# A graph network's edge loop: attribute products grouped behind the first transposes, message sums in one run behind the second product

## The chip, the cores and the metric

The kernel runs on one core of a Trainium2 chip. The metric is the device time of one execution in microseconds (us), the median of several runs. A core has five engines that each work through their own instructions in order and wait for one another by semaphores: PE (TensorE, matrix products), ACT (ScalarE, functions and copies), DVE (VectorE, elementwise work), POOL (GpSimd, which issues the gathers here) and SP (which issues plain transfers). PEld is TensorE's weight load, which runs beside its products. Products land in PSUM, a small memory from which ACT and DVE read.

## The reference

Four graph layers run one after the other on 4096 nodes of 512 features and 65,536 edges sorted by destination; each adds its result to the node features. Layer 2 passes messages along the edges, and its edge part is what matters here:

```python
def mish(x):
    return x * jnp.tanh(jax.nn.softplus(x))
edge_feat = jnp.concatenate([x[src], x[dst], edge_attr], axis=-1)
h = mish(edge_feat @ W1 + b1)
messages = mish(h @ W2 + b2)
agg = jax.ops.segment_sum(messages, dst, num_segments=x.shape[0])
```

`x` is normalized and rectified before; `edge_attr` has 64 numbers an edge. `agg` then goes through another small network over the nodes. All of it is fp32.

## The kernel before

The product with W1 is split by its three inputs. Two tables over the nodes, `ptab` (source part) and `qtab` (destination part, with b1), are made before the loop. The loop (function `messages`, L937 to L1089) then works through 128 groups of 512 edges. A group is four blocks (j = 0 to 3) of 128 edges, one edge on each partition. For a group it does the following:

- `fetch_rows` (L941) gathers four blocks of `ptab` rows by source into the tile `pg`, and `add_rows` (L947) gathers the `qtab` rows by destination on top of them. POOL issues these eight gathers. `pg` has four buffers.
- `fetch_attributes` (L905) loads the 64 attributes of the edges into `eg`, through SP's queue. `eg` has four buffers.
- `turn_attributes` (L954) transposes the attributes on PE, two blocks at a time (L957), and ACT copies them to `et` (L959).
- `attribute_products` (L962) multiplies one block's attributes by their rows of W1, `w1e`. The product has only 64 rows of depth, so blocks 0 and 2 use one half of TensorE's rows and blocks 1 and 3 the other (L967). DVE adds the result to the gathered rows (L1050, L1057).
- The first mish is worked out as h * cos(2 arctan(sigmoid(-h))), the cosine as a sine: Sigmoid (L1005), Arctan (L1024) and Sin (L1069) on ACT into the tile `qg`, and a multiplication on DVE in two halves (L1070, L1079). The first group has its own function for this, `first_mish` (L997). Sigmoid and Sin need different function tables, so ACT loads a table twice a group.
- `turn_h(j)` (L971) transposes one block of the result in four pieces (L974), and ACT copies it to `h_t` (L976).
- `second_product` (L979) multiplies it by W2 (`product`, L401) into `m_ps`. DVE adds b2 and so makes `z` (L1036, L1053, L1067, L1077). Products 0 to 3 below are those of blocks 0 to 3.
- The second mish is the same on `z`, with the tile `t` (L1028, L1046, L1063 on ACT, L1064, L1074 on DVE).
- `in_parts` (L984) splits the messages into two parts that a faster matrix format can hold, on DVE (L987, L988). `one_hots` (L404) compares each edge's local destination with 0 to 127 (L407).
- `add_messages` (L991) sums the messages by destination: a product of the one-hot matrix with the parts, two products a block (L994), into `sum_ps`. `add_window` (L420) adds this to the two blocks of nodes that the group can reach, in the accumulator `acc` (L424).

Several groups are under way at once. In step i the gathers of group i+2 are asked for, the attribute products belong to group i+1, the first mish to i, the second product to i-1 and the second mish to i-2. The order of the work is written out by hand: the loop stands under `manual_schedule`, which keeps the written order on PE, ACT, DVE and POOL. So each engine's list of instructions is the order of the statements in L1013 to L1090. PSUM tiles are `tr_ps` (two buffers, shared by both kinds of transposes), `small_ps` (three), `m_ps` (two) and `sum_ps` (one).

On PE, a step is written as: product 0, sums of blocks 2 and 3 of the group before, attribute transposes, `turn_h` 2 and 3, attribute products 0 and 1, product 1, attribute products 2 and 3, products 2 and 3, `turn_h` 0 and 1 of the next group, sums of blocks 0 and 1.

Of the kernel before, what the change touches and what calls it, by code (L numbers as in the profile page):

```python
# [34 lines left out]
def kernel(  # L35
# [891 lines left out]
    with ExitStack() as l2:  # L927
# [6 lines left out]
        w2_sb = load_w(wp, "w2_sb", w2)  # L934
        b2_bc = row_bc(wp, "b2_bc", b2)
        @with_exitstack
        def messages(ctx, fetched):  # L937
            lp = ctx.enter_context(tc.tile_pool(name="l2", bufs=2))
            lps = ctx.enter_context(tc.tile_pool(name="l2_ps", bufs=2, space=PSUM))

            def fetch_rows(i):  # L941
                pg = lp.tile([P, U, D], F32, name="pg", bufs=4)
                for j in range(U):
                    gather(pg[:, j, :], ptab, d_src[:, i * U + j:i * U + j + 1])
                return pg

            def add_rows(i, pg):  # L947
                for j in range(U):
                    t = i * U + j
                    nc.gpsimd.indirect_dma_start(  # L950
                        out=pg[:, j, :], out_offset=None, in_=qtab,
                        in_offset=bass.IndirectOffsetOnAxis(ap=d_dst[:, t:t + 1], axis=0), compute_op=OP.add)

            def turn_attributes(eg):  # L954
                et_ps = lps.tile([P, U // 2, P], F32, name="tr_ps")
                for j in range(U // 2):
                    nc.tensor.transpose(et_ps[:, j, :], eg[:, 2 * j:2 * j + 2, :].rearrange("q j d -> q (j d)"), ident)  # L957
                et = lp.tile([P, U // 2, P], F32, name="et")
                nc.scalar.copy(et, et_ps)  # L959
                return et  # L960

            def attribute_products(et, js):  # L962
                made = []
                for j in js:
                    ps = lps.tile([P, D], F32, name="small_ps", bufs=3)
                    half = slice((j % 2) * DE, (j % 2 + 1) * DE)
                    nc.tensor.matmul(ps, et[half, j // 2, :], w1e[half, :], start=True, stop=True)  # L967
                    made.append(ps)
                return made

            def turn_h(j, h):  # L971
                h_ps = lps.tile([P, KC, P], F32, name="tr_ps")
                for k in range(KC):
                    nc.tensor.transpose(h_ps[:, k, :], h[:, j, k * P:(k + 1) * P], ident)  # L974
                h_t = lp.tile([P, KC, P], F32, name="h_t", bufs=4)
                nc.scalar.copy(h_t, h_ps)  # L976
                return h_t

            def second_product(h_t):  # L979
                m_ps = lps.tile([P, D], F32, name="m_ps")  # L980
                product(m_ps, h_t, w2_sb)
                return m_ps

            def in_parts(m):  # L984

                parts = lp.tile([P, 2, 2, D], F32R, name="parts", bufs=2)
                nc.vector.tensor_copy(parts[:, 0], m)  # L987
                nc.vector.tensor_sub(parts[:, 1], m, parts[:, 0].bitcast(F32))  # L988
                return parts

            def add_messages(ps, js, oh, parts):  # L991
                for j in js:
                    for k in range(2):
                        nc.tensor.matmul(ps, oh[:, j, :], parts[j // 2][:, k, j % 2, :],  # L994
                                         start=j == 0 and k == 0, stop=j == U - 1 and k == 1)

            def first_mish(pg, qg):  # L997
                nc.scalar.activation(qg, qg, AF.Arctan)
                nc.scalar.activation(qg, qg, AF.Sin, bias=half_pi, scale=-2.0)
                nc.vector.tensor_mul(pg, pg, qg)  # L1000

            def begin_mish(i):
                h[i] = rows.pop(i)
                s = lp.tile([P, U, D], F32, name="qg", bufs=2)
                nc.scalar.activation(s, h[i], AF.Sigmoid, scale=-1.0)  # L1005
                return h[i], s

            fetched, rows, h, z, h_t = dict(fetched), {}, {}, {}, {}  # L1010
            pg, qg, left = None, None, None
            ctx.enter_context(tc.manual_schedule(engines=ENGINES))
            for i in range(-2, NG + 3):  # L1013
                now = lambda k: 0 <= k < NG
                if now(i + 2):
                    rows[i + 2] = fetch_rows(i + 2)
                if now(i + 3) and i + 3 not in fetched:
                    fetched[i + 3] = fetch_attributes(i + 3)
                if now(i + 2):
                    add_rows(i + 2, rows[i + 2])  # L1020
                if i == 0:
                    first_mish(pg, qg)
                if now(i) and i > 0:
                    nc.scalar.activation(qg, qg, AF.Arctan)  # L1024
                if now(i - 2):
                    mz = z.pop(i - 2)
                    t = lp.tile([P, U, D], F32, name="t", bufs=1)
                    nc.scalar.activation(t, mz, AF.Sigmoid, scale=-1.0)  # L1028
                if now(i - 1):
                    hh = h.pop(i - 1)  # L1030
                    zz = z[i - 1] = lp.tile([P, U, D], F32, name="z", bufs=2)
                    ps = second_product(h_t.pop(0))
                if left:
                    add_messages(left[1], (2, 3), *left[2:])
                if now(i - 1):
                    nc.vector.tensor_add(zz[:, 0, :], ps, b2_bc)  # L1036
                if left:
                    add_window(left[0], d_bi, d_half, row_at, left[1])
                    left = None
                if now(i + 1):  # L1040
                    et = turn_attributes(fetched.pop(i + 1))
                    nxt = rows[i + 1]
                if now(i - 1):
                    h_t[2], h_t[3] = turn_h(2, hh), turn_h(3, hh)
                if now(i - 2):
                    nc.scalar.activation(t, t, AF.Arctan)  # L1046
                if now(i + 1):
                    made = attribute_products(et, (0, 1))
                    for j in range(2):
                        nc.vector.tensor_add(nxt[:, j], nxt[:, j], made[j])  # L1050
                if now(i - 1):
                    ps = second_product(h_t.pop(1))
                    nc.vector.tensor_add(zz[:, 1, :], ps, b2_bc)  # L1053
                if now(i + 1):
                    made = attribute_products(et, (2, 3))
                    for j in range(2):
                        nc.vector.tensor_add(nxt[:, 2 + j], nxt[:, 2 + j], made[j])  # L1057
                if now(i - 1):
                    ps2 = second_product(h_t.pop(2))
                if now(i - 2):  # L1060
                    oh = one_hots(lp, d_loc, (i - 2) * U, U, bufs=1, dtype=F32R)
                if now(i - 2):
                    nc.scalar.activation(t, t, AF.Sin, bias=half_pi, scale=-2.0)  # L1063
                    nc.vector.tensor_mul(mz[:, :2], mz[:, :2], t[:, :2])  # L1064
                    parts = [in_parts(mz[:, :2])]
                if now(i - 1):
                    nc.vector.tensor_add(zz[:, 2, :], ps2, b2_bc)  # L1067
                if now(i) and i > 0:
                    nc.scalar.activation(qg, qg, AF.Sin, bias=half_pi, scale=-2.0)  # L1069
                    nc.vector.tensor_mul(pg[:, :2], pg[:, :2], qg[:, :2])  # L1070
                if now(i - 1):
                    ps = second_product(h_t.pop(3))
                if now(i - 2):
                    nc.vector.tensor_mul(mz[:, 2:], mz[:, 2:], t[:, 2:])  # L1074
                    parts.append(in_parts(mz[:, 2:]))
                if now(i - 1):
                    nc.vector.tensor_add(zz[:, 3, :], ps, b2_bc)  # L1077
                if now(i) and i > 0:
                    nc.vector.tensor_mul(pg[:, 2:], pg[:, 2:], qg[:, 2:])  # L1079
                last = pg  # L1080
                if now(i + 1):
                    pg, qg = begin_mish(i + 1)
                if now(i):
                    for j in range(2):
                        h_t[j] = turn_h(j, last)
                if now(i - 2):
                    left = i - 2, lps.tile([P, D], F32, name="sum_ps", bufs=1), oh, parts
                    add_messages(left[1], (0, 1), *left[2:])

        messages(begun)  # L1090

# [377 lines left out]
```

## Time and profile before

| | us |
|---|---|
| median of 3 runs (5613.23 to 5616.71) | 5616.13 |
| the profiled execution | 5951.3 |
| its span, first to last instruction | 5949.5 |
| regular part of the layer 2 edge loop in it | about 2086 to 4612 |
| one group there | 20.37 |

The page and the traces describe one execution under the profiler, which took 5.6% longer than the median. Times of single instructions come from it. In the rows, an instruction is named by line, engine, operation, and the tile it writes and reads; a row with xN merges N records, and an fp32 matrix product has two records. A line can be that of a helper: L401 are all second products in this loop, L407 all one-hots.

A busy engine is not an engine at its peak. The records of pipelined matrix products overlap, so a row's length is more than the time until the next product starts. The sums in the prediction therefore use the time from one start to the next.

### The profile page before, as it was taken

The page shows a single profiled execution, that of the slowest core. Times are in us where ns is not written, and L with a number is a line of the kernel's source. Part 1 is how long each engine was busy: PE and PEld are TensorE (multiplying, and loading weights), DVE is VectorE, ACT ScalarE, POOL GpSimd, SP SyncE. Part 2 cuts the span into 40 slices and gives each one's busy share as a digit, 9 for nine tenths or more (in the row PEclk, how much of TensorE's full clock was granted, in tenths as well). Part 3 has the DMA queues.
Part 4 walks back from the last instruction along what each step waited for, and adds up shares of the span by engine and source line. Part 5 has one row for each costly group of instructions (what it writes and reads, how often), then busy time and mean ns, then how long its engine had stood idle before and what let it go on. Part 6 is the DMA issues. An engine that isn't in the chain of part 4 may idle for free.

```text
span 5949.5 us, 56469 instructions
## 1 busy us (share of the span) xinstructions
PE 5249.2 (88%) x17274; PEld 2791.2 (47%) x17274; DVE 3558.3 (60%) x5695; ACT 3356.1 (56%) x5015; POOL 3082.0 (52%) x2604
## 2 busy tenths in 40 slices
PE   7677777869999799999999999999999899866676
PEld 4466666424444344444444444444444666522222
DVE  8566667623223377777777777777777565522323
ACT  1144445423433488888888888888888433333333
POOL 0266664066666465665565566566554111166665
PEclk9799999989999899999999999999999999988888
DMA  3366665467777555555555555555554212266775
GB/s 105 98 176 181 184 181 159 159 212 232 234 227 232 147 118 108 111 110 109 110 111 110 108 113 109 108 112 110 108 110 84 78 64 68 84 187 187 209 222 183
DMA packets 344871, 841.72 MB, mean 141 GB/s; under 512 B 60272, under 2 KB 76656, under 8 KB 344560
## 3 DMA queue, kind: packets, MB, share of 16 engines
q0 software_dynamic: 237568, 673.35, 46.8%
q1 hardware_dynamic: 106992, 164.66, 8.1%
q8 instruction: 141, 2.31, 0.2%
q14 instruction: 170, 1.39, 0.1%
HBM read 752.62 MB, written 85.20 MB: 141 GB/s over the span
## 4 chain that ended last, share of the span: by engine, by line
PE 75%; DVE 8%; another core or an unknown queue 6%; issue 4%; ACT 3%; DMA 2%; DVEq 1%; POOL 1%; SPq 0%; POOLq 0%; ACTq 0%
PE m_ps L401 30%; PE sum_ps L768 13%; PE small_ps L967 5%; PE tr_ps L974 4%; PE sum_ps L994 4%; PE pq_ps L868 4%; PE o_ps L401 4%; PE u_ps L1177 4%; PE sum_ps L684 4%; DVE rows L678 2%; DVE acc L424 1%; PE y_ps L401 1%; ACT oh L744 1%; POOL rows L412 1%
## 5 line engine op out<-in xcount | busy, mean ns | idle before, releaser
L401 PE MATMUL m_ps<-w_sb,h_t 128*128 128x512 f32 x4096 | 1848.0, 599 | 1.5 <-ACT h_t L976 1.5
L768 PE MATMUL sum_ps<-g,oh 128*128 128x512 f32 x2048 | 1012.2, 636 | 248.2 <-ACT oh L745 133.1
L401 PEld LDWEIGHTS m_ps<-w_sb,h_t 128*128 128x128 f32 x4096 | 757.1, 190 | 1002.9 <-issue 989.1
L950 POOL DMA_INDIRECT pg<-qtab,d_dst x512 | 1050.9, 2053 | 156.5 <-issue 155.4
L412 POOL DMA_INDIRECT pg<-ptab,d_src x512 | 498.5, 974 | 909.6 <-ACT h_t L976 726.4
L768 PEld LDWEIGHTS sum_ps<-g,oh 128*128 128x128 f32 x2048 | 412.1, 205 | 793.6 <-issue 600.2
L412 POOL DMA_INDIRECT rows<-htab,s_dst x512 | 484.1, 946 | 515.8 <-issue 360.1
L424 DVE SCALAR_TENSOR_TENSOR acc<-sum_ps,d_half,acc 128x512 f32 x512 | 384.6, 751 | 581.8 <-remote 241.3
L412 POOL DMA_INDIRECT g<-ytab,s_dst x512 | 484.9, 947 | 460.8 <-issue 326.9
L684 PE MATMUL sum_ps<-rows,oh 128*128 128x261 f32 x2048 | 528.2, 408 | 160.2 <-DVE rows L678 87.1
L412 POOL DMA_INDIRECT g<-ztab,d_src x512 | 486.6, 950 | 324.5 <-issue 142.7
L424 DVE SCALAR_TENSOR_TENSOR acc<-sum_ps,s_half,acc 128x522 f32 (+1 forms) x256 | 193.6, 756 | 575.1 <-PE sum_ps L768 275.7
L684 PEld LDWEIGHTS sum_ps<-rows,oh 128*128 128x128 f32 x2048 | 392.5, 199 | 249.5 <-DVE rows L678 101.1
L976 ACT COPY h_t<-tr_ps 128x512 f32<-128x512 f32 x512 | 287.2, 588 | 338.8 <-PE tr_ps L974 314.2
L994 PE MATMUL sum_ps<-parts,oh 128*128 128x512 f32 x1024 | 344.1, 457 | 12.4 <-DVE parts L987 10.7
L868 PE MATMUL pq_ps<-w_sb,ht_mid 128*128 128x512 f32 x512 | 272.2, 619 | 58.7 <-ACT ht_mid L863 58.7
L988 DVE TENSOR_TENSOR parts<-z,parts 128x1024 fp32r<-128x1024 f32 x256 | 313.9, 1226 | 8.7
L967 PE MATMUL small_ps<-w1e,et 64*128 64x512 f32 x1024 | 295.3, 648 | 20.8 <-ACT et L959 13.0
L744 ACT ACTIVATE oh<-row_i,d_loc 128x128 f32<-128x128 f32 x512 | 162.2, 387 | 249.5 <-remote 149.1
L974 PE MATMUL tr_ps<-ident,pg 128*128 128x128 f32 x2048 | 297.4, 278 | 3.9 <-DVE pg L1070 0.6
L974 PEld LDWEIGHTS tr_ps<-ident,pg 128*128 128x128 f32 x2048 | 224.6, 142 | 118.7 <-issue 84.5
L1168 POOL TENSOR_TENSOR h_sb<-h_sb,b_bc 128x1024 f32<-128x1024 f32 x16 | 37.7, 2357 | 453.5 <-PE tr L1152 358.0
(283 smaller groups left out, 7937.7 us busy)
## 6 DMA issues: line engine op xcount, KB each, us to landing
xt<-in_x_dram SPq DMA_DIRECT2D x16, 1024.0 KB
eg<-in_edge_attr_dram SPq DMA_DIRECT2D x128, 128.0 KB
htab<-acc SPq DMA_DIRECT2D x32, 256.0 KB
rows<-htab,s_dst POOLq DMA_INDIRECT x512
x<-xt SPq DMA_DIRECT2D x8, 1024.0 KB
ytab<-acc SPq DMA_DIRECT2D x32, 256.0 KB
x_mid<-x SPq DMA_DIRECT2D x32, 256.0 KB
g<-ytab,s_dst POOLq DMA_INDIRECT x512
```

Of the source, the lines that this page charges most:

```text
L401: nc.tensor.matmul(ps, h_t[:, k, :], w_sb[:, k0 + k, :], start=start and k == 0, stop=stop and k == KC - 1)
L412: nc.gpsimd.indirect_dma_start(out=dst_ap, out_offset=None, in_=table, in_offset=bass.IndirectOffsetOnAxis(ap=idx, axis=0))
L424: nc.vector.scalar_tensor_tensor(at, ps, half[:, k, i:i + 1], at, op0=OP.mult, op1=OP.add)
L684: nc.tensor.matmul(ps[:, c, :HW], oh[:, j + k, :], rows[:, j + k, c * HW:(c + 1) * HW], start=j + k == 0, stop=j + k == GT - 1)
L768: nc.tensor.matmul(ps, oh[:, j, :], g[:, j, :], start=i % per == 0 and j == 0, stop=i % per == per - 1 and j == U - 1)
L868: nc.tensor.matmul(ps, h_t[:, k, :], self.w1_sb[:, k0 + k, :], start=k == 0, stop=k == KC - 1)
L950: nc.gpsimd.indirect_dma_start(out=pg[:, j, :], out_offset=None, in_=qtab, in_offset=bass.IndirectOffsetOnAxis(ap=d_dst[:, t:t + 1], axis= ...
L967: nc.tensor.matmul(ps, et[half, j // 2, :], w1e[half, :], start=True, stop=True)
L974: nc.tensor.transpose(h_ps[:, k, :], h[:, j, k * P:(k + 1) * P], ident)
L976: nc.scalar.copy(h_t, h_ps)
L988: nc.vector.tensor_sub(parts[:, 1], m, parts[:, 0].bitcast(F32))
L994: nc.tensor.matmul(ps, oh[:, j, :], parts[j // 2][:, k, j % 2, :], start=j == 0 and k == 0, stop=j == U - 1 and k == 1)
```

## The change

Six things change, all in `messages`:

- All four attribute products of a group stand together, after `turn_h` 0 and 1. `small_ps` gets a fourth buffer.
- `turn_attributes` follows them, for the group after that one, so `et` is made a step earlier. Attributes are fetched a step earlier too.
- `turn_h` 0 and 1 move from the end of a step to the start of the next, and `turn_h` 2 and 3 now follow product 0.
- The eight sums of a group stand together, between products 1 and 2, in a `small_ps` buffer; `sum_ps` is gone. They belong to group i-3 instead of i-2. The splits and the one-hots move with them, to the first half of the step.
- The b2 addition of block 3 moves to the start of the next step.
- `first_mish` is gone; the first group takes the same way as the others. The two halves of the first mish's multiplication on DVE now stand together.

No instruction of the regular part is added or removed, only moved. On PE, a step becomes: `turn_h` 0 and 1, attribute products 0 to 3, attribute transposes, product 0, `turn_h` 2 and 3, product 1, the eight sums, products 2 and 3.

```diff
             def attribute_products(et, js):
...
-                    ps = lps.tile([P, D], F32, name="small_ps", bufs=3)
+                    ps = lps.tile([P, D], F32, name="small_ps", bufs=4)
...
-            pg, qg, left = None, None, None
+            qg, ps3 = None, None
...
-                if now(i + 3) and i + 3 not in fetched:
-                    fetched[i + 3] = fetch_attributes(i + 3)
+                if now(i + 4) and i + 4 >= len(begun):
+                    fetched[i + 4] = fetch_attributes(i + 4)
                 if now(i + 2):
                     add_rows(i + 2, rows[i + 2])
-                if i == 0:
-                    first_mish(pg, qg)
-                if now(i) and i > 0:
+                if now(i - 1):
+                    hh = h.pop(i - 1)
+                    h_t[0], h_t[1] = turn_h(0, hh), turn_h(1, hh)
+                if now(i - 2):
+                    nc.vector.tensor_add(z[i - 2][:, 3, :], ps3, b2_bc)
+                if now(i):
                     nc.scalar.activation(qg, qg, AF.Arctan)
+                if now(i + 1):
+                    nxt = rows[i + 1]
+                    for j, ps in enumerate(attribute_products(et.pop(i + 1), range(U))):
+                        nc.vector.tensor_add(nxt[:, j], nxt[:, j], ps)
+                if now(i + 2):
+                    et[i + 2] = turn_attributes(fetched.pop(i + 2))
+                if now(i - 1):
+                    ps = second_product(h_t.pop(0))
                 if now(i - 2):
-                    mz = z.pop(i - 2)
+                    mz = z[i - 2]
                     t = lp.tile([P, U, D], F32, name="t", bufs=1)
                     nc.scalar.activation(t, mz, AF.Sigmoid, scale=-1.0)
+                if now(i - 3):
+                    done = z.pop(i - 3)
+                    parts = [in_parts(done[:, :2]), in_parts(done[:, 2:])]
                 if now(i - 1):
-                    hh = h.pop(i - 1)
                     zz = z[i - 1] = lp.tile([P, U, D], F32, name="z", bufs=2)
-                    ps = second_product(h_t.pop(0))
-                if left:
-                    add_messages(left[1], (2, 3), *left[2:])
-                if now(i - 1):
                     nc.vector.tensor_add(zz[:, 0, :], ps, b2_bc)
-                if left:
-                    add_window(left[0], d_bi, d_half, row_at, left[1])
-                    left = None
-                if now(i + 1):
-                    et = turn_attributes(fetched.pop(i + 1))
-                    nxt = rows[i + 1]
+                if now(i - 3):
+                    oh = one_hots(lp, d_loc, (i - 3) * U, U, bufs=1, dtype=F32R)
                 if now(i - 1):
                     h_t[2], h_t[3] = turn_h(2, hh), turn_h(3, hh)
                 if now(i - 2):
                     nc.scalar.activation(t, t, AF.Arctan)
-                if now(i + 1):
-                    made = attribute_products(et, (0, 1))
-                    for j in range(2):
-                        nc.vector.tensor_add(nxt[:, j], nxt[:, j], made[j])
                 if now(i - 1):
                     ps = second_product(h_t.pop(1))
                     nc.vector.tensor_add(zz[:, 1, :], ps, b2_bc)
-                if now(i + 1):
-                    made = attribute_products(et, (2, 3))
-                    for j in range(2):
-                        nc.vector.tensor_add(nxt[:, 2 + j], nxt[:, 2 + j], made[j])
-                if now(i - 1):
-                    ps2 = second_product(h_t.pop(2))
-                if now(i - 2):
-                    oh = one_hots(lp, d_loc, (i - 2) * U, U, bufs=1, dtype=F32R)
+                if now(i - 3):
+                    ps = lps.tile([P, D], F32, name="small_ps", bufs=4)
+                    add_messages(ps, range(U), oh, parts)
+                    add_window(i - 3, d_bi, d_half, row_at, ps)
                 if now(i - 2):
                     nc.scalar.activation(t, t, AF.Sin, bias=half_pi, scale=-2.0)
                     nc.vector.tensor_mul(mz[:, :2], mz[:, :2], t[:, :2])
-                    parts = [in_parts(mz[:, :2])]
                 if now(i - 1):
-                    nc.vector.tensor_add(zz[:, 2, :], ps2, b2_bc)
-                if now(i) and i > 0:
+                    ps = second_product(h_t.pop(2))
+                if now(i):
                     nc.scalar.activation(qg, qg, AF.Sin, bias=half_pi, scale=-2.0)
-                    nc.vector.tensor_mul(pg[:, :2], pg[:, :2], qg[:, :2])
-                if now(i - 1):
-                    ps = second_product(h_t.pop(3))
+                    for k in range(2):
+                        half = slice(2 * k, 2 * k + 2)
+                        nc.vector.tensor_mul(h[i][:, half], h[i][:, half], qg[:, half])
                 if now(i - 2):
                     nc.vector.tensor_mul(mz[:, 2:], mz[:, 2:], t[:, 2:])
-                    parts.append(in_parts(mz[:, 2:]))
                 if now(i - 1):
-                    nc.vector.tensor_add(zz[:, 3, :], ps, b2_bc)
-                if now(i) and i > 0:
-                    nc.vector.tensor_mul(pg[:, 2:], pg[:, 2:], qg[:, 2:])
-                last = pg
+                    nc.vector.tensor_add(zz[:, 2, :], ps, b2_bc)
+                    ps3 = second_product(h_t.pop(3))
                 if now(i + 1):
-                    pg, qg = begin_mish(i + 1)
-                if now(i):
-                    for j in range(2):
-                        h_t[j] = turn_h(j, last)
-                if now(i - 2):
-                    left = i - 2, lps.tile([P, D], F32, name="sum_ps", bufs=1), oh, parts
-                    add_messages(left[1], (0, 1), *left[2:])
+                    qg = begin_mish(i + 1)
```

More of the change, by code (lines that the diff above doesn't have):

```diff
@@ L936, in messages @@
         @with_exitstack
-        def messages(ctx, fetched):
+        def messages(ctx, begun):
             lp = ctx.enter_context(tc.tile_pool(name="l2", bufs=2))
@@ L995, in add_messages @@
                                          start=j == 0 and k == 0, stop=j == U - 1 and k == 1)
[L997 to L1000, printed above, removed]
             def begin_mish(i):
@@ L1005, in begin_mish @@
                 nc.scalar.activation(s, h[i], AF.Sigmoid, scale=-1.0)
-                return h[i], s
-            fetched, rows, h, z, h_t = dict(fetched), {}, {}, {}, {}
-            pg, qg, left = None, None, None
+                return s
+            fetched, rows, h, z, h_t, et = dict(begun), {}, {}, {}, {}, {}
+            qg, ps3 = None, None
             ctx.enter_context(tc.manual_schedule(engines=ENGINES))
```

## The prediction

> **What bounds the kernel now.** I began with the page's sections 1 and 4, to see which engine the end hangs on:
>
> ```profile
> span 5949.5 us, 56469 instructions
> PE 5249.2 (88%) x17274; PEld 2791.2 (47%) x17274; DVE 3558.3 (60%) x5695; ACT 3356.1 (56%) x5015; POOL 3082.0 (52%) x2604
> ...
> PE 75%; DVE 8%; another core or an unknown queue 6%; issue 4%; ACT 3%; DMA 2%; DVEq 1%; POOL 1%; SPq 0%; POOLq 0%; ACTq 0%
> ```
>
> TensorE carries 75% of the chain, but only the layer 2 edge loop changes. So next, the busy time of that loop's regular part, 2100 to 4600 us:
>
> ```profile
> 2100.00:4600.00 2500.00, 2496.83 (x8107) 1216.65 (x8106) 1920.46 (x2335) 2026.64 (x1597) 1480.98 (x972) 1.00 0.55 109
> ```
>
> The columns are PE, PEld, DVE, ACT, POOL, clock, DMA share. PE is busy 99.9% at full clock; DVE has 23% idle, ACT 19%. But "busy" overlaps pipelined matmuls, so it hides what is lost between them. For that, the PE timeline of one group, from its first transposes to those of the next:
>
> ```profile
> 3002.60 1.06 PE L974 MATMUL tr_ps<-ident,pg 128*128 128x128 f32 x8
> 3003.41 1.18 PE L994 MATMUL sum_ps<-parts,oh 128*128 128x512 f32 x4
> 3004.43 3.60 PE L401 MATMUL m_ps<-w_sb,h_t 128*128 128x512 f32 x8
> 3007.47 1.49 PE L994 MATMUL sum_ps<-parts,oh 128*128 128x512 f32 x4
> 3008.79 0.38 PE L957 MATMUL tr_ps<-ident,eg 128*128 128x128 f32 x2
> 3009.01 1.28 PE L974 MATMUL tr_ps<-ident,pg 128*128 128x128 f32 x8
> 3010.22 1.13 PE L967 MATMUL small_ps<-w1e,et 64*128 64x512 f32 x4
> 3011.28 3.70 PE L401 MATMUL m_ps<-w_sb,h_t 128*128 128x512 f32 x8
> 3014.91 1.13 PE L967 MATMUL small_ps<-w1e,et 64*128 64x512 f32 x4
> 3015.97 7.13 PE L401 MATMUL m_ps<-w_sb,h_t 128*128 128x512 f32 x16
> 3022.96 0.30 PE L974 MATMUL tr_ps<-ident,pg 128*128 128x128 f32 x1
> ```
>
> The period is 3022.96 - 3002.60 = 20.36 us; an fp32 matmul is two records. From starts of single records in this trace: m_ps 0.429 us a record, a transpose 0.109, a sum 0.233, a pair of attribute records (two 64-row halves at once) 0.429 once running. The work alone is 32 x 0.429 + 18 x 0.109 + 8 x 0.233 + 4 x 0.429 = 13.73 + 1.96 + 1.86 + 1.72 = 19.27 us. So 1.09 us a group is lost. The loop's waits say where:
>
> ```profile
> PEld m_ps L401 <- issue: 949.4, 3437, 0.8
> ...
> PEld small_ps L967 <- issue: 113.1, 245, 0.8
> ...
> PEld tr_ps L974 <- ACT et L959: 32.1, 123, 0.3
> ```
>
> The long first row is mostly the 0.24 us by which a weight load is early. The 0.8 us maxima on L967 and L401 are the change to 64-row matmuls and back; the last row is turn_h(3) waiting for the attribute copy.
>
> **What the Trainium skill says.** "TensorEngine Tiling (Array Packing)", Key Properties: changing the tiling mode drains TensorE. The trace agrees and gives the price. The visit at 3014.91: record starts 14.388 to 14.911 = 0.523 (0.094 over the 0.429 pitch), 0.533 for the first pair (+0.104), 0.519 back to m_ps (+0.090), 0.533 for the first m_ps record (+0.104): 0.39 us. The visit at 3010.22, entered from transposes: 0.40. "TensorE: Matmul & The Clock Gate", Architectural detail, has ScalarE and VectorE as strict FIFOs, so a waiting instruction holds all behind it; the ACT and DVE rows here are in written order. "PSUM — Partial Sum Buffer", Specifications: 8 banks of 512 fp32. The loop uses 2 tr_ps + 3 small_ps + 2 m_ps + 1 sum_ps = 8, afterwards 2 + 4 + 2 = 8 (no trace shows banks).
>
> **The change part by part**, against one period; T is the start of turn_h(0).
>
> (a) Attribute products: one visit per group instead of two, between transposes. Removed: 0.39 + 0.40 = 0.79. Added: 0.094 + 0.104 + 0.090 and 0.03 to 0.10 for the first transpose after it, so 0.32 to 0.39; I take 0.35. That four in a row run at one pair per 0.429 after the first is seen at the loop's start, at half clock: starts 39.732, 40.747, 41.600, 42.453 after 2000, i.e. 1.02, then 0.85 and 0.85.
>
> (b) Attribute transposes come a group early, and turn_h(2), turn_h(3) follow product 0. turn_h(3) no longer waits for the copy `et`: its stall is 9.336 to 9.634 = 0.298 instead of 0.109, then 0.166, together 0.25 us. In the new order `et` is copied at about T+3.7 to T+4.2 (behind Arctan), and turn_h(3) comes at T+7.1. Removed 0.25. If that cover failed, 0.25 would stay.
>
> (c) New seams: m_ps to transposes twice instead of once, +0.05 (0.451 and 0.135 against 0.429 and 0.109). Transposes to m_ps twice: not in the regular trace. Nearest is transposes to sums, 0.345 for 0.109 + 0.233, nothing; the other end is a weight load of 0.19 behind a transpose of 0.109, 0.08 each. No reason for a gain. I take 0.04 each, 0.08.
>
> (d) Sums x8 in one run: today's two runs already take 8 x 0.233 plus nothing; 0.
>
> Sum: 0.79 + 0.25 - 0.35 - 0.05 - 0.08 = 0.56 us; ends 0.44 (0.39 and 0.16 taken) and 0.72 (0.32, 0, 0). New period about 19.8.
>
> This holds if nothing else is late. I replayed one group with this trace's start-to-start times. PE: first products at T+0.9, `et` transposes 2.8, product 0 3.1, turn_h(2, 3) 6.7, product 1 7.6, sums 11.1, products 2 and 3 12.9 to 19.8. ACT: copies 0.7 to 1.8, Arctan 3.7, `et` 4.2, Sigmoid t 6.1; copies 7.4 to 8.6, Arctan t 10.5, table 11.8, Sin t 13.7, Sin q 15.7, table 17.0, Sigmoid 18.9; it must be free by T+20.5. DVE: four attribute adds (0.64) from 2.2 to 4.8, two casts and subtractions (0.73 + 1.14 each) to 8.5, z0 and one-hots (0.61 each) to 9.7; z1 at 11.4, window 13.2 to 14.8, then mul z, h, h, z (1.14 each) 15.9, 17.0, 18.2, 19.3, z2 19.9. Needed: sums at 11.1 (margin 1.4), the next turn_h(0) at 19.8 (margin 2.8), product 0 with z2's bank at 22.9 (3.0). Added waits, with products 2 and 3 and the next transposes queued behind: the sums' wait for one-hots, parts and their small_ps buffer. The buffer was read by the first add at T+2.9. A fourth attribute product reuses the last sum's buffer, free at T+14.8 of the group before.
>
> Gathers: POOL refills a pg buffer after turn_h(3), now at T+7.6; the rows are needed two periods less 5.4 us later, 34 us (42 before). Issue takes 14.3 us and landing about 4 (first at the loop's start: issued until 2021.8, used 2025.6). Margin 15 us; each us beyond it would cost a us a group, 124 us. SP fetches attributes with the same four buffers a group earlier and uses them a group earlier: nothing.
>
> The first group's multiplication (2.29 us) becomes two halves and the next group's adds stand before it, once, at a start that waits for gathers in any case: nothing.
>
> Whole loop: 124 regular periods (turn_h starts 2086.14 to 4611.56) x 0.56 = 69 us. The start is set by gathers landing in both: 0. At the end the last group's one-hots (0.6) and four more sums at the cold pitch seen there (about 0.4 each) come after its last split: +2. Net -67. Profiled execution: 5951.3 - 67 = 5884. The median is 335 us lower than that execution; nothing shown says where. The loop is at full clock and bound by TensorE, so I carry the 67 us over undiminished: 5616 - 67 = 5549.
>
> **The rivals.** (R1) ACT's wait comes back in another place, since the `et` copy now stands behind a 1.92 us Arctan, and both new seams cost 0.08 with the higher drain: 0.44 - 0.25 = 0.19 x 124 = 24, less 2: 5594. For it: today's stall is of this kind. Against: the 3 us margin. (R2, slower) DVE comes late to the sums: adds, splits, z0 and one-hots are one unbroken run of 7.5 us in order ahead of them, and PE then stands idle with products 2 and 3 behind. The margin is 1.4 us, so it decides once that run takes over 1.4 + 0.56 = 2.0 us longer; at 2.5 us longer each group loses 0.54, 67 us plus 2: 5685. For it: today this work is scattered, and DVE is only just in time elsewhere: turn_h(0)'s weight load starts at 3022.93, held until L1070 ends at 3022.81. Against: every step has its duration from a row here, and DVE is 77% busy. (R3) The parts cancel: some 5616. That the order isn't what is written is excluded by the manual schedule; the built program has the four products behind the first transposes and the eight sums behind product 1.
>
> **How the numbers follow.** Forecast, 0.44 to 0.72 a group: 0.66, own range 5525 to 5565. R1 and like partial losses (5566 to 5604): 0.14. R3, within 0.2% (11 us, about what a measurement of this kernel can tell from no change): 0.06. R2: 0.14. So faster 0.80, same 0.06, slower 0.14. The range 5518 to 5612 leaves out R2, half of R3 and a little below, about 0.19.
>
> **What would show it.** The period between turn_h(0) starts 19.6 to 19.9; L967 in runs of eight records lasting about 1.9 us to the next transpose; L974's wait for `et` gone; DVE's one-hots ended more than 1 us before the sums. Wrong would be: PE idle before L994 or L974 released by DVE, a clock below 1.00 in the loop, or L1026 waiting for gathers.

## The result, and the profile after

The changed kernel takes 5521.61 us (median of 4 runs, 5521.04 to 5524.6), the kernel before 5615.69 beside it: 94 us less, ratio 0.9834 with a 95% interval of 0.9817 to 0.9851. Forecast were 5549 and 67 us less. The sign and the place were right; the gain is 1.4 times the one forecast, and a group gains 0.75 us, just above the 0.44 to 0.72 of the forecast.

The profiled execution of the changed kernel has a span of 5522.8 us. The busy times of the loop's regular part in it (columns as before: PE, PEld, DVE, ACT, POOL, clock, DMA share):

```profile
1900.00:4200.00 2300.00, 2300.00 (x7738) 1187.35 (x7737) 1809.61 (x2228) 1902.13 (x1525) 1264.23 (x939) 1.00 0.57 114
```

TensorE is still the engine without a pause, at full clock. As before, that says nothing about the gaps between starts. The PE timeline of one group after the change does:

```profile
3006.05 1.04 PE L974 MATMUL tr_ps<-ident,pg 128*128 128x128 f32 x8
3007.02 1.99 PE L967 MATMUL small_ps<-w1e,et 64*128 64x512 f32 x8
3008.94 0.44 PE L957 MATMUL tr_ps<-ident,eg 128*128 128x128 f32 x2
3009.21 3.60 PE L401 MATMUL m_ps<-w_sb,h_t 128*128 128x512 f32 x8
3012.65 1.04 PE L974 MATMUL tr_ps<-ident,pg 128*128 128x128 f32 x8
3013.52 3.60 PE L401 MATMUL m_ps<-w_sb,h_t 128*128 128x512 f32 x8
3016.55 2.39 PE L994 MATMUL small_ps<-parts,oh 128*128 128x512 f32 x8
3018.78 7.03 PE L401 MATMUL m_ps<-w_sb,h_t 128*128 128x512 f32 x16
3025.65 0.60 PE L974 MATMUL tr_ps<-ident,pg 128*128 128x128 f32 x4
```

The period (from one turn_h(0) to the next) is 3025.65 - 3006.05 = 19.60 us, where it was 20.36; over the regular part the means are 19.61 and 20.37. The eight attribute records form one run of 3008.94 - 3007.02 = 1.92 us (about 1.9 forecast). turn_h(2, 3) takes 13.52 - 12.65 = 0.87 where it took 1.21: the stall is gone. The waits of the weight loads say the same by what is missing:

```profile
PEld m_ps L401 <- issue: 730.1, 3052, 0.2
PEld tr_ps L974 <- issue: 123.3, 468, 0.3
PEld tr_ps L957 <- issue: 88.7, 117, 0.8
PEld small_ps L967 <- issue: 74.6, 351, 0.2
PEld small_ps L994 <- issue: 56.0, 234, 0.2
```

The row of L974 waiting for `et` is gone, and the maxima of 0.8 on L967 and L401 are gone. One 0.8 is left, on L957: the way back from the only visit of 64-row products. No row names DVE or ACT. Such a table doesn't show every short wait, as e7 below will tell; here the starts of single records confirm it at both entries of turn_h and at both ways from transposes to m_ps, where all steps are within 0.003 us of the plain pitches.

The profiled execution of the kernel before was 335 us above its median (6.0% of the median, not the 5.6% given above), that of the changed kernel was not; the first experiment looks into that. Runs e4 to e6 were made in slow executions of this kind, with the kernel before at 5947.34 us beside them, and are read by their ratio to it, by the loop's length and by the period.

### The profile page after: what moved, and what is told of

It reads as the page before. It is cut to its first block, busy times and chain, and to the rows that moved or that the text cites. A ratio compares the mean times of both kernels' runs of the same rounds, so it can differ in the third digit from the quotient of the medians.

```text
span 5522.8 us, 56347 instructions
## 1 busy us (share of the span) xinstructions
PE 5110.0 (93%) x17274; PEld 2739.2 (50%) x17274; DVE 3529.2 (64%) x5696; ACT 3323.5 (60%) x5015; POOL 2910.0 (53%) x2604
## 3 DMA queue, kind: packets, MB, share of 16 engines
q14 instruction: 170, 1.39, 0.1%
## 4 chain that ended last, share of the span: by engine, by line
PE 69%; DMA 6%; POOL 4%; issue 2%; DVE 1%; ACT 1%; DVEq 0%; SPq 0%; POOLq 0%; ACTq 0%
PE m_ps L401 32%; PE sum_ps L768 9%; DMA g<-ztab,d_src 5%; PE small_ps L967 4%; PE small_ps L994 4%; PE o_ps L401 4%; PE tr_ps L974 4%; PE u_ps L1159 4%; PE pq_ps L868 4%; POOL g L412 4%; PE tr_ps L957 1%; PE tr L1134 1%; PE y_ps L401 1%; DMA g<-ytab,s_dst 0%; ACT h_t L1136 0%
## 5 line engine op out<-in xcount | busy, mean ns | idle before, releaser
L401 PE MATMUL m_ps<-w_sb,h_t 128*128 128x512 f32 x4096 | 1820.8, 592 | 0.5 <-ACT h_t L976 0.5
L401 PEld LDWEIGHTS m_ps<-w_sb,h_t 128*128 128x128 f32 x4096 | 757.5, 190 | 809.1 <-issue 797.8
L950 POOL DMA_INDIRECT pg<-qtab,d_dst x512 | 880.7, 1720 | 156.4 <-issue 144.1
L768 PEld LDWEIGHTS sum_ps<-g,oh 128*128 128x128 f32 x2048 | 355.7, 191 | 745.0 <-issue 342.4
L684 PE MATMUL sum_ps<-rows,oh 128*128 128x261 f32 x2048 | 502.8, 393 | 98.7 <-DVE rows L678 98.7
L424 DVE SCALAR_TENSOR_TENSOR acc<-sum_ps,d_half,acc 128x512 f32 x256 | 192.3, 751 | 444.8 <-PE sum_ps L768 425.6
L1026 DVE TENSOR_TENSOR pg<-pg,small_ps 128x512 f32<-128x512 f32 x512 | 318.6, 683 | 186.7 <-PE small_ps L967 150.1
L994 PE MATMUL small_ps<-parts,oh 128*128 128x512 f32 x1024 | 310.7, 446 | 13.4 <-DVE oh L407 13.4
L974 PEld LDWEIGHTS tr_ps<-ident,pg 128*128 128x128 f32 x2048 | 240.6, 142 | 145.6 <-issue 145.6
L424 DVE SCALAR_TENSOR_TENSOR acc<-small_ps,d_half,acc 128x512 f32 x256 | 192.3, 751 | 171.6 <-PE small_ps L994 152.3
L1063 DVE TENSOR_TENSOR pg<-pg,qg 128x1024 f32<-128x1024 f32 x256 | 301.4, 1219 | 0.7 <-ACT qg L1060 0.7
L974 PE MATMUL tr_ps<-ident,pg 128*128 128x128 f32 x2048 | 266.3, 273 | 10.8 <-DVE pg L1063 10.8
```

Source lines behind the costliest of these rows:

```text
L401: nc.tensor.matmul(ps, h_t[:, k, :], w_sb[:, k0 + k, :], start=start and k == 0, stop=stop and k == KC - 1)
L424: nc.vector.scalar_tensor_tensor(at, ps, half[:, k, i:i + 1], at, op0=OP.mult, op1=OP.add)
L684: nc.tensor.matmul(ps[:, c, :HW], oh[:, j + k, :], rows[:, j + k, c * HW:(c + 1) * HW], start=j + k == 0, stop=j + k == GT - 1)
L768: nc.tensor.matmul(ps, oh[:, j, :], g[:, j, :], start=i % per == 0 and j == 0, stop=i % per == per - 1 and j == U - 1)
L950: nc.gpsimd.indirect_dma_start(out=pg[:, j, :], out_offset=None, in_=qtab, in_offset=bass.IndirectOffsetOnAxis(ap=d_dst[:, t:t + 1], axis= ...
L1026: nc.vector.tensor_add(nxt[:, j], nxt[:, j], ps)
```

## The experiments

**e0: the kernel before once more**, for a second profile. No edit.

> The kernel before, once more, for a second profile of it. Both theories: a group of the layer 2 edge loop takes 20.37 us as in the first profile, and the run takes about 5616 us. The first profile's 335 us above the median should then be missing, and missing outside the loop.

Measured: 5613.6 us, ratio 1.0 (0.9991 to 1.001), span 5608.8. Busy times by stage, the first profile of the kernel before (layer 0's edges, layer 1's edges, the layer 2 edge loop and, after "...", layer 3's edges):

```profile
256.00:1028.00 772.00, 595.83 (x3048) 478.02 (x3048) 513.43 (x885) 361.71 (x1399) 472.15 (x500) 0.93 0.63 174
1197.00:2011.00 814.00, 712.43 (x1682) 313.92 (x1682) 245.36 (x518) 305.85 (x786) 479.88 (x509) 0.95 0.72 218
2015.00:4672.00 2657.00, 2620.48 (x8479) 1276.78 (x8480) 2002.14 (x2432) 2121.48 (x1670) 1552.67 (x1026) 0.99 0.55 111
...
5193.00:5949.00 756.00, 514.72 (x1024) 212.86 (x1024) 211.61 (x288) 253.85 (x663) 486.61 (x512) 0.85 0.67 200
```

and the same stages in the second:

```profile
256.00:898.00 642.00, 542.85 (x3044) 447.24 (x3043) 513.50 (x895) 366.62 (x1408) 470.86 (x498) 0.99 0.75 211
1066.00:1770.00 704.00, 681.14 (x1678) 306.47 (x1676) 245.40 (x518) 305.83 (x786) 478.07 (x505) 0.99 0.80 250
1774.00:4431.00 2657.00, 2619.01 (x8479) 1277.26 (x8480) 2002.01 (x2432) 2122.29 (x1671) 1552.88 (x1026) 0.99 0.54 111
...
4950.00:5608.00 658.00, 538.44 (x1024) 163.59 (x1024) 211.51 (x288) 256.72 (x663) 485.81 (x512) 0.98 0.77 230
```

The loop takes 2657 us in both. The three other edge stages, each with gathers and a DMA share of 0.63 or more, make up 130 + 110 + 98 = 338 us. The granted clock in them was 0.85 to 0.95 in the first profile and 0.98 to 0.99 in the second; what lowered it isn't shown. So carrying the loop's gain over to the median undiminished was right.

**e1: the products split again in the changed kernel.**

```diff
-                    nxt = rows[i + 1]
-                    for j, ps in enumerate(attribute_products(et.pop(i + 1), range(U))):
+                    nxt, near = rows[i + 1], et.pop(i + 1)
+                    for j, ps in enumerate(attribute_products(near, (0, 1))):
                         nc.vector.tensor_add(nxt[:, j], nxt[:, j], ps)
...
                     nc.vector.tensor_add(zz[:, 1, :], ps, b2_bc)
+                if now(i + 1):
+                    for j, ps in enumerate(attribute_products(near, (2, 3))):
+                        nc.vector.tensor_add(nxt[:, 2 + j], nxt[:, 2 + j], ps)
```

> The changed kernel with attribute products 2 and 3 behind product 1 again, a second visit of 64-row products per group. Theory (the gain is mostly what TensorE lost at seams): the visit costs about 0.39 us a group as it did before, x 124 = 48 us, so about 5570 us. Rival (the gain comes from the slack that a later group gives DVE and ACT, not from joining the products): within 10 us of the changed kernel, 5522 us.

Measured: 5570.35 us, ratio to the kernel before 0.9921 (0.9904 to 0.9937); 49 us above the changed kernel. The period is 20.02 us, 0.40 more. The second visit on its timeline:

```profile
3017.08 3.60 PE L401 MATMUL m_ps<-w_sb,h_t 128*128 128x512 f32 x8
3020.61 1.13 PE L967 MATMUL small_ps<-w1e,et 64*128 64x512 f32 x4
3021.67 1.67 PE L994 MATMUL small_ps<-parts,oh 128*128 128x512 f32 x6
```

The eight m_ps records now take 20.61 - 17.08 = 3.53 to the next start where eight pitches are 3.43, the two pairs 1.06 instead of 0.86, and the eight sums together take 0.1 longer. That is the 0.40 of the period, and the theory's price holds; the rival's "within 10 us" does not.

**e2: in the kernel before, the four products joined at the first place.**

```diff
-                    ps = lps.tile([P, D], F32, name="small_ps", bufs=3)
+                    ps = lps.tile([P, D], F32, name="small_ps", bufs=4)
...
-                    made = attribute_products(et, (0, 1))
-                    for j in range(2):
+                    made = attribute_products(et, range(U))
+                    for j in range(U):
                         nc.vector.tensor_add(nxt[:, j], nxt[:, j], made[j])
...
-                if now(i + 1):
-                    made = attribute_products(et, (2, 3))
-                    for j in range(2):
-                        nc.vector.tensor_add(nxt[:, 2 + j], nxt[:, 2 + j], made[j])
...
-                    left = i - 2, lps.tile([P, D], F32, name="sum_ps", bufs=1), oh, parts
+                    left = i - 2, lps.tile([P, D], F32, name="small_ps", bufs=4), oh, parts
```

> The kernel before with the four attribute products joined at the first place (small_ps of four buffers, the sums in it too), nothing else moved. Theory: one visit of 0.39 us less a group, x 124 = 48 us, so about 5568 us; the wait of turn_h(3) for the attribute copy stays. Rival: no gain without the later group, 5616 us.

Measured: 5555.75 us, ratio 0.9895 (0.9878 to 0.9911), 59 us less; the period is 19.91, 0.45 less. By record starts, 0.40 of it is the visit and 0.05 lies at the end of products 2 and 3, where the next group's transposes come in (0.01 more in the sums); e7 follows the 0.05 up.

**e3: in the kernel before, the attribute transposes a group earlier**, behind products 0 and 1.

```diff
-                if now(i + 3) and i + 3 not in fetched:
-                    fetched[i + 3] = fetch_attributes(i + 3)
+                if now(i + 4) and i + 4 >= 3:
+                    fetched[i + 4] = fetch_attributes(i + 4)
...
-                    et = turn_attributes(fetched.pop(i + 1))
+                    et = ets.pop(i + 1)
...
                         nc.vector.tensor_add(nxt[:, j], nxt[:, j], made[j])
+                if now(i + 2):
+                    ets[i + 2] = turn_attributes(fetched.pop(i + 2))
```

> The kernel before with the attribute transposes a group earlier and behind products 0 and 1, nothing else moved. Theory: the stall of turn_h(3) goes (0.25 us) and the first visit is left into transposes instead of m_ps (0.40 becomes about 0.33), together 0.32 us x 124 = 40 us, so about 5576 us. Rival (the stall only moves to the next wait, DVE's): within 10 us of 5616 us.

Measured: 5586.7 us, ratio 0.9952 (0.9935 to 0.9968), 28 us less; the period is 20.13, 0.23 less instead of 0.32. turn_h(2, 3) goes from 1.21 to 0.97, as expected, and the way back into transposes saves 0.04 instead of 0.07. But the step at the end of products 2 and 3 grows by another 0.06. So the rival was right on a part: TensorE would come to turn_h(0) earlier, but DVE's multiplication (L1070 in the kernel before) again ends only 0.15 us ahead of it, as in the kernel before.

**e4: both edits of e2 and e3 in the kernel before**, the messages summed as before.

> The kernel before with the products joined and the attribute transposes behind them a group earlier, but the messages summed as before (same group, two runs, on either side of product 0). Theory: 0.39 + 0.25 + 0.07 = 0.71 us a group of the 0.77 gained, x 124 = 88 us, so about 5528 us, 6 us above the changed kernel; moving the messages is worth little. Rival (the later group matters as much): 5550 us or more.

Measured: 5857.08 us, ratio 0.9851 (0.9826 to 0.9876), 90 us less than the kernel before there. The period is 19.62, and the loop, from its first gather to the first product of the stage after it, takes 2563.1 us. In the kernel before that is 2656.8, in the changed kernel 2562.2. From its PE timeline of one group:

```profile
3006.88 1.17 PE L994 MATMUL small_ps<-parts,oh 128*128 128x512 f32 x4
...
3010.92 1.49 PE L994 MATMUL small_ps<-parts,oh 128*128 128x512 f32 x4
...
3013.21 1.99 PE L967 MATMUL small_ps<-w1e,et 64*128 64x512 f32 x8
3015.13 0.44 PE L957 MATMUL tr_ps<-ident,eg 128*128 128x128 f32 x2
```

One visit, between transposes, and the sums in two runs on either side of product 0. The whole gain of the change is there without its second half. It is 0.746 us a group, more than the theory's 0.71, because the 0.05 at turn_h(0) goes here too.

**e5 and e6: DVE made late in the changed kernel**, by one and by two unused multiplications ahead of z0 and the one-hots (`range(2)` in e6).

```diff
                     parts = [in_parts(done[:, :2]), in_parts(done[:, 2:])]
+                    for _ in range(1):
+                        spare = lp.tile([P, 2, D], F32, name="spare", bufs=1)
+                        nc.vector.tensor_mul(spare, done[:, :2], done[:, 2:])
```

> The changed kernel with one unused multiplication of 128x1024 (1.14 us from start to start) on DVE behind the splits, ahead of z0 and the one-hots. In the changed kernel's profile the one-hots end 1.17 us before the sums could start. Theory (TensorE alone bounds the loop, DVE has this margin): no change, 5522 to 5527 us. Rival (DVE bounds the loop somewhere, or nearly so): about 1 us a group, 5640 us.

> The same with two of these multiplications, 2.28 us. Theory: 2.28 - 1.17 = 1.1 us of lateness a group, x 125 = 138 us, so about 5660 us, and TensorE idle before the sums with DVE's one-hots as releaser. Rival (DVE's lateness is made up elsewhere in the group): within 20 us of 5522 us.

Measured: e5 5872.55 us, ratio 0.9884 (0.9855 to 0.9912), period 19.75, 0.13 more than the changed kernel; e6 6029.58 us, ratio 1.0146 (1.0115 to 1.0176), period 21.01, 1.39 more. The waits of PE and of the weight loads in e6:

```profile
PE small_ps L994 <- DVE oh L407: 117.4, 105, 1.5
```

```profile
PEld small_ps L994 <- DVE oh L407: 204.3, 105, 2.3
```

The mechanism is the theory's, its margin is not: e5 should have changed nothing and loses 0.13 us a group. Counted from turn_h(0), the one-hots end at T+9.730 in the changed kernel, T+10.865 in e5 and T+12.124 in e6, so they are 1.135 and 2.394 us later (the second multiplication costs more than the 1.14 expected). Both points give the same margin: 1.135 - 0.135 = 1.00 and 2.394 - 1.394 = 1.00, not the 1.17 us from the one-hots' end to the first sum. The last 0.17 us are needed for the weight load of the first sum: in the changed kernel it starts with the last m_ps record, 0.43 us before the sum; in e5 and e6 it starts 0.05 us after the one-hots. With the margin gone, DVE's lateness becomes the loop's one for one.

**e7: two DVE instructions exchanged in the kernel before**, to learn what the step at turn_h(0) is.

```diff
-                if now(i - 1):
-                    nc.vector.tensor_add(zz[:, 2, :], ps2, b2_bc)
                 if now(i) and i > 0:
                     nc.scalar.activation(qg, qg, AF.Sin, bias=half_pi, scale=-2.0)
                     nc.vector.tensor_mul(pg[:, :2], pg[:, :2], qg[:, :2])
+                if now(i - 1):
+                    nc.vector.tensor_add(zz[:, 2, :], ps2, b2_bc)
```

> The kernel before with two DVE instructions exchanged: the first half of the first mish's multiplication now stands ahead of z2. The question is what the step from the last second product to the first transposes costs in the kernel before (0.05 us more than the plain pitches). Theory: it is no seam of TensorE but a wait for that multiplication, which ends 0.6 us earlier here; so a group takes 20.32 instead of 20.37 us and the run 6 us less, 5608 where the kernel before takes 5614. Rival (a seam of TensorE's own): 20.37 us a group, no change.

Measured: 5607.69 us, ratio 0.9987 (0.9981 to 0.9994), the kernel before 5614.59: 7 us less. The period is 20.31, 0.06 less: 0.05 at turn_h(0) and 0.01 in the sums. DVE's multiplication and the weight load of turn_h(0), in the kernel before and in e7:

```profile
3021.60 1.21 DVE L1070 TENSOR_TENSOR pg<-pg,qg 128x1024 f32<-128x1024 f32 x1
3022.93 0.31 PEld L974 LDWEIGHTS tr_ps<-ident,pg 128*128 128x128 f32 x3 [0.66 <-issue]
```

```profile
3006.30 1.22 DVE L1068 TENSOR_TENSOR pg<-pg,qg 128x1024 f32<-128x1024 f32 x1
3007.81 0.14 PEld L974 LDWEIGHTS tr_ps<-ident,pg 128*128 128x128 f32 x1 [0.24 <-issue]
```

In e7 the load starts 0.43 us before the transposes at 3008.24. In the kernel before it starts only 0.03 us before those at 3022.96, 0.12 us behind the end of L1070, and the profile puts the delay down to "issue", not to DVE. So it was a wait for DVE, and no seam.

**e8 and e9: the changed kernel and e4's kernel side by side.**

> The changed kernel again, beside the next one on the same chip. Both theories: 19.61 us a group, ratio to the kernel before 0.983 or 94 us less.

> The kernel before with products joined and attribute transposes behind them, messages summed as before, beside the changed kernel on the same chip. Theory (moving the messages is worth nothing): 19.62 us a group and a time within 5 us of the changed kernel. Rival (the later group is worth something that the trace of one group doesn't show, at the loop's ends or elsewhere): 10 us or more above it.

Measured: e8 5519.16 us, ratio 0.9829 (0.9816 to 0.9842); e9 5521.07 us, ratio 0.9834 (0.982 to 0.9847). The periods are 19.61 and 19.62. The two can't be told apart: the medians differ by 1.9 us, less than the runs of each among themselves. e9 has none of the change but the joined products and the earlier attribute transposes, so moving and joining the messages, with all that moved along with them, brings no time here.

Whether it brings or costs DVE room is another question, and these runs don't settle it. In e9's trace the multiplication ends at 3021.36, 0.52 us before the transposes of turn_h(0) at 3021.88:

```profile
3020.14 1.21 DVE L1068 TENSOR_TENSOR pg<-pg,qg 128x1024 f32<-128x1024 f32 x1
```

In the kernel before, 0.15 us there meant a wait; in the changed kernel its first half ends 2.8 us ahead. The sums are the other way round: their inputs are ready 2.6 us or more ahead in e9, 1.17 in the changed kernel. So room has moved from the sums to turn_h(0), and no run with a later DVE in e9 tells which kernel bears more.

## Why the prediction was right, and where its sum was off

The mechanism stands, but for part (c): TensorE bounds the loop, its pure work doesn't change, and the gain is what it lost at seams and waits. 124 periods times 20.367 - 19.613 = 0.754 us are 93.5 us of the 94 measured. The terms, in us a group:

| term of the forecast | forecast | measured |
|---|---|---|
| (a) two visits of 64-row products become one | 0.79 - 0.35 = 0.44 | 0.800 - 0.353 = 0.447 |
| (b) turn_h(3) no longer waits for `et` | 0.25 | 0.246 |
| (c) m_ps to transposes, one seam more | -0.05 | 0.000 |
| (c) transposes to m_ps, two seams | -0.08 | -0.008 |
| the step from products 2 and 3 to turn_h(0), taken as unchanged | 0.00 | 0.049 |
| (d) sums in one run | 0.00 | 0.019 |
| sum | 0.56 | 0.753 (0.754 by the periods) |

The measured terms are means over the regular groups of both profiles, from starts of single records.

(a) In the changed kernel the visit costs 0.094 on entry, 0.202 in its four pairs and on leaving, and 0.057 on the first transpose: 0.353, the 0.35 that the forecast took. Counted the same way, each of the two visits before costs 0.40. The forecast had 0.39 for the one between m_ps records, since its four steps left out the 0.007 us between the two records of a pair. The price was confirmed both ways, by e1 (+0.40) and e2 (0.40 of its 0.45).

(b) Confirmed alone by e3: turn_h(2, 3) 0.25 shorter.

(c) This is the step that failed. I read 0.451 and 0.135 at the entry of turn_h(0) as the price of going from m_ps to transposes, and charged it once more for the second entry. In the changed kernel both entries show the plain 0.429 and 0.109. The excess was a wait: turn_h(0) for the multiplication of L1070. e7 removes it by DVE's order alone; e3 doubles it (to 0.11), since TensorE would be there sooner; in e2 it goes because DVE's attribute adds then stand earlier, and in the changed kernel the multiplication itself comes earlier. The forecast had even seen that L1070 ended only 0.12 us before that weight load, and used it as an argument for R2, but not to split the 0.05. The other seam, from transposes to m_ps, was charged at 0.04 each (half of the 0.08 by which a weight load is longer than a transpose), and that was not there either: 0.110 and 0.431 in place of 0.109 and 0.429. This could have been seen before. At the end of the loop, where no attribute products follow, the kernel before goes from turn_h(2, 3) straight to m_ps, and its eight transposes take 4636.77 - 4635.90 = 0.87 us, which is 8 x 0.109:

```profile
4635.90 1.03 PE L974 MATMUL tr_ps<-ident,pg 128*128 128x128 f32 x8
4636.77 10.47 PE L401 MATMUL m_ps<-w_sb,h_t 128*128 128x512 f32 x24
```

So 0.13 was charged and 0.01 due, and 0.05 was gained that had been counted as fixed. The forecast's upper end of 0.72 had both new seams at nothing already; what it still lacked is this wait, and 0.02 in the sums.

(d) and the title's second half: e9 shows by the whole time, and e4 by the loop's length, that they bring nothing that can be told from the time. Why the eight sums run 0.02 us shorter together isn't shown.

The replay of the other engines held. The first sum was set at T+11.1 and really comes at 3016.95 - 3006.05 = T+10.9 (one pitch of 0.429 after the last m_ps start, 3016.53; its own record is drawn from 3016.55 on and is longer by as much); the one-hots were set to end at T+9.7 and end there. DVE in the changed kernel:

```profile
3008.18 2.48 DVE L1026 TENSOR_TENSOR pg<-pg,small_ps 128x512 f32<-128x512 f32 x4 [1.14 <-PE small_ps L967]
...
3015.10 0.68 DVE L407 TENSOR_TENSOR oh<-row_i,d_loc 128x512 fp32r<-128x512 f32 x1
```

What was too kind is the margin: 1.4 us in the forecast, 1.0 by e5 and e6. R2, the slower case, is thus a real danger and starts nearer than I had put it: by an estimate from these runs, 1.0 + 0.75 us of lateness undo the gain (2.0 in the forecast), and e6, with 2.39, is indeed slower than the kernel before. Nothing in the changed kernel itself brings that about. R1 didn't occur: `et` is copied by 3009.84, T+3.8, and turn_h(3) needs it at T+7.1.

The loop's end was forecast 2 us longer. From the last group's first transposes to the next stage's first it is 4666.71 - 4629.71 = 37.0 us before and 4337.28 - 4298.56 = 38.7 after; eight sums now stand there alone behind the one-hots.

## What to carry to other kernels

When one engine bounds a loop, make its account from the starts of its records: pure pitches first, then what each change of neighbour costs over them; here that found 1.09 us in a loop that showed as 99.9% busy. Before an excess is called the price of a seam, look what ended just before that start on the engines it waits for: an excess that repeats exactly can still be a wait, even one that the profile puts down to "issue", and the test is an edit on the other engine's order alone. Look too for a place outside the regular loop where the new neighbours already stand together. And of a change with two halves, try each half: here one carried the whole gain, and the other brought no time; whether it leaves DVE more margin or less stays open.

## What the runs showed of the hardware that was not expected

- A visit of 64-row products costs less between transposes (0.35 us) than between fp32 products of 512 columns (0.40 us): the first full-height instruction afterwards loses 0.06 instead of 0.10.
- Going between transposes and fp32 products of 512 columns costs next to nothing in either direction as long as no wait holds the weight load: 0.429, 0.109, 0.110, 0.431 at the seams.
- A one-hot matrix had to be done 0.17 us before the start of the sums that load it as weights (1.17 by starts against a margin of 1.00 in e5 and in e6). A load that isn't held started 0.43 us ahead, with the m_ps record before it (changed kernel, e7).
